# One graph layer and one graph-attention layer on one core: x1 is transposed on VectorE and through DRAM instead of on TensorE, the third weight product moves into the front part, and GpSimd's sums get a fixed order

## The chip, the cores and the metric

The kernel runs on one core of one Trainium2 chip. The metric is the device time of one execution in microseconds (us); less is better. The engines are called PE (TensorE, the matrix engine; PEld are its weight loads), DVE (VectorE), ACT (ScalarE), POOL (GpSimd) and SP (SyncE, which here issues all DMAs). Each engine works through its own queue in order. Which instruction stands where in a queue is decided when the program is built.

## The reference

There are 64 graphs of 256 nodes with 512 features, all fp32. Two layers follow each other, each with a residual and a layer norm:

```
h  = relu(adj @ (x @ W1) + b1)
h  = relu(adj @ (h @ W2) + b2)
x1 = layernorm(x + adj @ (h @ W3) + b3)

q, k = split(x1 @ Wqk);  v = x1 @ Wv
agg  = adj @ (k * mask)
w    = mask * sum(q * agg, -1) / sqrt(512)        # one number per node
out  = layernorm(x1 + softmax(w)[:, None] * v)
```

The kernel never forms q and k. With M = Wq Wk' it uses sum(q * agg) = sum((x1 M) * (adj (mask x1))), so that the second layer needs one weight product with M, one with Wv, and one product of the adjacency with mask * x1.

## The kernel before

**Tiling.** Two graphs (G = 2) are worked on together; there are 32 such pairs. A pair's features or nodes lie on the 128 partitions. Every large product is cut into 2 x 2 blocks and done with seven block products instead of eight. `seven` (L95) holds the schedule of one such group: the products are issued in the order 1, 7, 6, 2, 5, 3, 4 into three PSUM banks called x (products 1, 6, 5, 3 add up in it), v (7 and 4) and y (2). Between the products ACT copies partial results out of x (t1 after product 1, u after 6, q after 5), and DVE adds a bank and a copy into the four output blocks (c11 after 2, c22 after 5, c21 after 4; c12 after 3 is an ACT copy or a DVE add). The operands of products 3, 5, 6 and 7 include sums of blocks:

- `a_sums` (L207) makes four sums S of blocks of the left operand on POOL, 128 x 512 each. Product 7 needs S[2]; product 6 needs S[1], which is made from S[0].
- `b_sums` (L80) makes four sums T of blocks of the right operand, also 128 x 512: for weights once on DVE, for data on POOL. Product 7 needs T[2]; product 6 needs T[1], which is made from T[0].

**Stages of one pair.** `support` (L219) is a weight product: 28 matmuls (56 passes on PE, since each fp32 matmul is two) of 128 x 256, on line L227. `aggregate` (L233) multiplies by the adjacency without the seven-product trick: 32 passes into four PSUM banks (L240), each emptied by one ACT instruction with bias and relu (L243) into a feature chunk of hT. `adj_times` (L257) multiplies by the adjacency with seven products (28 passes, L265). `front` does support 1, aggregate 1, support 2, aggregate 2. `back` does support 3, `adj_times` on its result C, the residual and the layer norm into r (this is x1), then 16 transposes of 128 x 128 on PE (L352) with four ACT copies (L353) to get x1T, then xm = mask * x1 on ACT (L359, four instructions), `adj_times` on xm into gt, and for each of the two graphs `attention` (L367): seven products of 128 x 512 against Wv and M with lhsT blocks of x1T or of its sums S, and the score w on DVE. `finish` (L394) waits for the softmax of w, forms the output on DVE (two fused multiply-adds and a layer norm per graph) and stores it.

**Order of the work.** `run` (L402) interleaves front of pair i with back of pair i - 1: both are generators, the one with fewer steps so far goes next, and `yield 8` (L346) after the layer norm of r keeps back still for eight steps of front. The instructions then go through a list scheduler that fills each engine's queue by priority and by its own estimate of when operands are ready, for all five engines. `softmax_rows`, `softmax_cols` and `finish` of pair i - 2 are called at the start and in the middle of support 3 of pair i - 1.

**Buffers.** PSUM has eight banks in one rotation. On-chip buffers of interest: S 6, act (hT and x1T) 5, r 2, x (shared by x and xm) 1, gt 1, v 3, T 4, tmp 6.

## Time and profile before

| | us |
|---|---|
| median of 3 runs (2920.73 to 2921.39) | 2920.84 |
| the profiled execution | 2920.62 |
| its span, first to last instruction | 2918.8 |
| PE busy in the span | 2883.0 (99%) |
| POOL / DVE / ACT busy | 1346.4 / 1009.2 / 911.4 |
| one pair in the steady part, start to start | 89.37 |

A row "PE MATMUL ... x28" stands for 28 passes, and its time runs from the first start to the modelled end of the last; the distance from one row's start to the next row's start is what PE really took. An idle time in brackets at the end of a row is that of the engine just before it, with what ended it. The steady part consists of 31 equal periods: the first pair alone (with the making of M) takes until 68.45, the periods until 2838.9, and the last pair's back, with nothing beside it, takes the rest.

### The profile page before, as it was taken

How to read it: one execution, taken by the hardware profiler on the slowest of the kernel's cores; microseconds unless marked ns; L12 is line 12 of the kernel's file. 1: busy time of each engine (PE TensorE's matmuls, PEld its weight loads, DVE VectorE, ACT ScalarE, POOL GpSimd, SP SyncE). 2: the span in 40 equal slices, each digit the busy share in tenths (PEclk: the TensorE clock that was granted, in tenths of full speed). 3: DMA queues.
4: the chain of work that ended last, by engine and by line, in shares of the span. 5: the costliest groups of instructions: out<-in, count | busy, mean ns of one | idle time of the engine just before them, and what ended most of it. 6: DMA issues, size and time to landing. Idle time of an engine off the chain costs nothing. (4 is left out here: it accounts for less than half of the span.)

```text
span 2918.8 us, 30346 instructions
## 1 busy us (share of the span) xinstructions
PE 2883.0 (99%) x11776; PEld 2150.7 (74%) x11776; DVE 1009.2 (35%) x2126; ACT 911.4 (31%) x1574; POOL 1346.4 (46%) x1130
## 2 busy tenths in 40 slices
PE   8999999999999999999999999999999999999996
PEld 7787777877777777778777787777787777877773
DVE  2233323333333333233333333332333333333325
ACT  2332333323333323333223333233332323332332
POOL 5534445444455344544444543545444445435442
PEclk9999999999999999999999999999999999999999
DMA  4101101111011011010110110110101101101000
GB/s 149 37 29 51 51 22 51 42 39 51 22 51 51 29 51 45 28 51 32 48 51 22 51 51 29 51 38 35 51 29 51 51 22 51 51 29 51 37 15 29
DMA packets 28719, 126.01 MB, mean 43 GB/s; under 512 B 3232, under 2 KB 6432, under 8 KB 20384
## 3 DMA queue, kind: packets, MB, share of 16 engines
q1 hardware_dynamic: 28576, 124.08, 11.7%
q8 instruction: 93, 1.52, 0.2%
q14 instruction: 50, 0.41, 0.0%
HBM read 90.51 MB, written 33.55 MB: 43 GB/s over the span
## 5 line engine op out<-in xcount | busy, mean ns | idle before, releaser
L227 PE MATMUL ps<-w_T,S 128*128 128x256 f32 x2304 | 524.0, 379 | 2.2 <-DVE w_T L85 1.6
L227 PEld LDWEIGHTS ps<-w_T,S 128*128 128x128 f32 x2304 | 437.5, 190 | 63.1 <-POOL S L61 2.7
L240 PE MATMUL ps<-aT,sup 128*128 128x256 f32 x2048 | 484.0, 381 | 0.0
L240 PEld LDWEIGHTS ps<-aT,sup 128*128 128x128 f32 x2048 | 386.4, 190 | 61.8 <-DVE sup L58 10.6
L373 PE MATMUL ps<-mv_T,S 128*128 128x512 f32 x768 | 350.5, 592 | 0.0
L58 DVE TENSOR_TENSOR sup<-ps,tmp 128x512 f32<-128x512 f32 x288 | 194.1, 683 | 441.1 <-PE ps L227 396.8
L243 ACT ACTIVATE hT<-ps,b 128x512 f32<-128x512 f32 x256 | 176.0, 688 | 441.6 <-PE ps L240 441.6
L111 ACT COPY tmp<-ps 128x512 f32<-128x512 f32 x224 | 131.3, 586 | 523.9 <-PE ps L227 290.8
L373 PEld LDWEIGHTS ps<-mv_T,S 128*128 128x128 f32 x768 | 145.9, 190 | 183.7 <-issue 168.6
L102 ACT COPY tmp<-ps 128x512 f32<-128x512 f32 x224 | 130.2, 581 | 401.4 <-PE ps L227 212.0
L119 ACT COPY tmp<-ps 128x512 f32<-128x512 f32 x224 | 130.7, 584 | 399.1 <-PE ps L373 180.5
L373 PE MATMUL ps<-v,x1T 128*128 128x512 f32 x512 | 251.0, 592 | 0.0
L227 PE MATMUL ps<-w,hT 128*128 128x256 f32 x1024 | 245.2, 382 | 0.0
L83 POOL TENSOR_TENSOR T<-sup 128x512 f32<-128x512 f32 x32 | 40.7, 1271 | 436.3 <-ACT sup L229 436.3
L61 POOL TENSOR_TENSOR S<-hT 128x512 f32<-128x512 f32 x128 | 162.5, 1270 | 144.7 <-PE ps L373 104.7
L58 DVE TENSOR_TENSOR v<-ps,tmp 128x512 f32<-128x512 f32 x128 | 88.5, 691 | 405.5 <-PE ps L373 405.5
L58 DVE TENSOR_TENSOR gt<-ps,tmp 128x512 f32<-128x512 f32 x96 | 66.4, 692 | 414.2 <-PE ps L265 388.6
L227 PEld LDWEIGHTS ps<-w,hT 128*128 128x128 f32 x1024 | 189.6, 190 | 24.5
L58 DVE TENSOR_TENSOR r<-ps,tmp 128x512 f32<-128x512 f32 x96 | 65.3, 680 | 407.6 <-PE ps L265 270.5
L265 PE MATMUL ps<-T,aS 128*128 128x256 f32 x768 | 197.0, 386 | 3.5 <-POOL T L85 3.5
L227 PE MATMUL ps<-w,S 128*128 128x256 f32 x768 | 179.1, 382 | 1.5 <-ACT tmp L119 0.8
L83 POOL TENSOR_TENSOR T<-xm 128x512 f32<-128x512 f32 x32 | 40.8, 1274 | 285.4 <-ACT xm L359 277.5
(94 smaller groups left out, 4059.0 us busy)
## 6 DMA issues: line engine op xcount, KB each, us to landing
xT<-in_xT SPq DMA_DIRECT2D x32, 1024.0 KB, 4.7
x<-in_xN SPq DMA_DIRECT2D x32, 1024.0 KB, 4.8
out<-v SPq DMA_DIRECT2D x64, 512.0 KB, 2.6
aT<-in_adjT SPq DMA_DIRECT2D x32, 512.0 KB, 5.4
w<-in_W SPq DMA_DIRECT2D x9, 256.0 KB, 5.2
wqT<-in_WqT SPq DMA_DIRECT2D x4, 256.0 KB, 5.2
wkT<-in_WkT SPq DMA_DIRECT2D x4, 256.0 KB, 5.0
v<-in_Wv SPq DMA_DIRECT2D x2, 512.0 KB, 6.4
```

Source lines behind the costliest of these rows:

```text
L58: nc.vector.tensor_tensor(o, a, b, op=OP.add)
L61: nc.gpsimd.tensor_tensor(o, a, b, op=op)
L83: eng.tensor_tensor(Ts[0], B[1], B[0], op=sub)
L102: nc.scalar.copy(t1, x)
L111: nc.scalar.copy(u, x)
L119: nc.scalar.copy(q, x)
L227: nc.tensor.matmul(ps[:, g], lhsT=src[n](c, g), rhs=w[n][:, c], start=(first and g == 0 and c == 0), stop=(g == G - 1 and c == 1), skip_gr ...
L240: nc.tensor.matmul(ps[:, g], lhsT=C[k][c // 2][:, g, (c % 2) * P:(c % 2 + 1) * P], rhs=aT[:, k, g], start=(g == 0 and k == 0), stop=(g == ...
L243: nc.scalar.activation(hT[c // 2][:, c % 2], ps, AF.Relu, bias=b[:, c:c + 1])
L265: nc.tensor.matmul(ps[:, g], lhsT=aS[n][:, g], rhs=mov[n][:, g], start=(first and g == 0), stop=(g == G - 1), skip_group_check=True)
L373: nc.tensor.matmul(ps, lhsT=src[n](c, g), rhs=mv[n][:, c], start=(first and c == 0), stop=(c == 1), skip_group_check=True)
```

## The change

- x1T is no longer made by PE. After the layer norm of each graph, four `nc.vector.transpose` instructions on DVE turn 128 x 256 of r each in blocks of 32 x 32 (eight per pair) into tr. One DMA writes tr (1 MB) to DRAM, four DMAs of 256 KB each read it back into 32 partitions of x1T each. In x1T neighbouring nodes lie 16 elements apart, so the attention's weight loads and the sums S of x1T read with that step. tr shares its one buffer with gt.
- Support 3, the sums of the adjacency (`adj_sums`), the load of x and x + b3 move from back to front; so do the sums S of the next pair's input. Back now begins with the sums T of C, then softmax and finish of the pair before, then `adj_times` on C.
- `run` now counts microseconds: each yield gives a stage's PE time (1.73, 0.86, 1.72), a tuple such as `(14,)` keeps the generator still for that long, and the generator that is further behind relative to 50 or 37 goes next.
- `manual_schedule` takes POOL out of the list scheduler: its queue has the order in which the code issues. In `b_sums` T[2] is made first.
- Buffers: S 11, act 4, r 1, v 2, x1T its own 1; the softmax works in place.

In the built program of the changed kernel DVE has eight `StreamTranspose` per pair, PE no longer has the 16 transposes, and SP has five more DMAs per pair.

```diff
+    dram = ctx.enter_context(tc.tile_pool(name="dram", bufs=2, space=bass.MemoryType.DRAM))
+    ctx.enter_context(tc.manual_schedule(engines={mybir.EngineType.Pool}))
...
     def b_sums(B, Ts, eng):
         sub = OP.subtract
+        eng.tensor_tensor(Ts[2], B[3], B[1], op=sub)
         eng.tensor_tensor(Ts[0], B[1], B[0], op=sub)
         eng.tensor_tensor(Ts[1], B[3], Ts[0], op=sub)
-        eng.tensor_tensor(Ts[2], B[3], B[1], op=sub)
         eng.tensor_tensor(Ts[3], B[2], Ts[1], op=sub)
...
-    def a_sums(hT):
-        S = [pool.tile([P, 2, G, P], FP, name="S", tag="S", bufs=6) for _ in range(4)]
-        blk = lambda h, k: hT[k][:, :, :, h * P:(h + 1) * P]
+    def a_sums(blk):
+        S = [pool.tile([P, 2, G, P], FP, name="S", tag="S", bufs=11) for _ in range(4)]
...
+    def first_sums(hT):
+        return a_sums(lambda h, k: hT[k][:, :, :, h * P:(h + 1) * P])
...
+    def t_sums(B):
         Ts = [pool.tile([P, G, HD], FP, name="T", tag="T", bufs=4) for _ in range(4)]
         b_sums((B[0][0], B[0][1], B[1][0], B[1][1]), Ts, nc.gpsimd)
+        return Ts
...
-    def front(i, hT, aT):
-        C = yield from support(hT, wl[0])
+    def front(i, hT, src, aT):
+        C = yield from support(hT, wl[0], src)
         nxt = load_xT(i + 1) if i + 1 < NPAIR else None
         hT = yield from aggregate(C, aT, bcol[0])
         C = yield from support(hT, wl[1])
         hT = yield from aggregate(C, aT, bcol[1])
-        return hT, nxt
-
-    def back(i, hT, aT, prev):
         x = load_x(i)
-        if prev is not None:
-            sm = softmax_rows(prev[2])
-        src = support(hT, wl[2])
-        for _ in range(3):
-            next(src)
-            yield
+        aS = adj_sums(aT)
+        steps = support(hT, wl[2])
+        for _ in range(4):
+            yield next(steps)
         for g in range(G):
             for h in range(NH):
                 padd(x[:, g, h, :], x[:, g, h, :], b3b)
+        nS = first_sums(nxt) if nxt is not None else None
+        C = yield from steps
+        return C, aS, x, nxt, nS
+
+    def back(i, C, aS, x, prev):
+        Ts = t_sums(C)
+        yield (3.4,)
         if prev is not None:
+            sm = softmax_rows(prev[2])
+            yield (3.4,)
             s = softmax_cols(sm)
             for g in range(G):
                 finish(i - 1, g, prev, s)
-        C = yield from src
-        aS = adj_sums(aT)
-        r = pool.tile([P, G, NH, D], FP, name="r", bufs=2)
+        r = pool.tile([P, G, NH, D], FP, name="r", bufs=1)
...
+        tr = pool.tile([P, 4, 32, NH, 2, 2, G], FP, name="tr", tag="gt", bufs=1)
+        x1T = pool.tile([P, P, NH, 2, 2, G], FP, name="x1T", bufs=1)
         for g in range(G):
             layernorm(r[:, g])
-        yield 8
-        x1T = [pool.tile([P, 2, G, N], FP, name="x1T", tag="act", bufs=5) for _ in range(2)]
-        for c in range(DC):
-            pt = bank()
-            for g in range(G):
-                for h in range(NH):
-                    nc.tensor.transpose(pt[:, g, h * P:(h + 1) * P], r[:, g, h, c * P:(c + 1) * P], ident)
-            nc.scalar.copy(x1T[c // 2][:, c % 2], pt)
-        yield
+            for h in range(NH):
+                for k in range(2):
+                    nc.vector.transpose(tr[:, :, :, h, k, :, g].rearrange("p q j c -> p c q j"),
+                                        r[:, g, h, k * HD:(k + 1) * HD].rearrange("p (c q j) -> p c q j", c=2, q=4))
+        via = dram.tile([4, P, D], FP, name="via")
+        nc.sync.dma_start(via.rearrange("q p e -> p q e"), tr.rearrange("p q j h k c g -> p q (j h k c g)"))
+        for q in range(4):
+            nc.sync.dma_start(x1T[q * 32:(q + 1) * 32].rearrange("p (a j) h k c g -> p a (j h k c g)", a=4),
+                              via[q].rearrange("(a i) e -> i a e", a=4))
+        yield (14,)
         xm = pool.tile([P, G, NH, D], FP, name="xm", tag="x", bufs=1)
...
-        yield from adj_times(aS, xmb, lambda y, t: add(gb(0, 0), y, t), lambda x: nc.scalar.copy(gb(0, 1), x),
+        yield from adj_times(aS, xmb, t_sums(xmb), lambda y, t: add(gb(0, 0), y, t), lambda x: nc.scalar.copy(gb(0, 1), x),
                              lambda v, t: add(gb(1, 0), v, t), lambda v, t: add(gb(1, 1), v, t))
+        src = a_sums(lambda h, k: x1T[:, :, h, k].rearrange("p n c g -> p c g n"))
+        yield (4,)
         for g in range(G):
             yield from attention(g)
...
     def run(*gens):
         res = [None] * len(gens)
-        live = {k: 0 for k in range(len(gens))}
+        done, free = [0.0] * len(gens), [0.0] * len(gens)
+        live = set(range(len(gens)))
+        now = 0.0
         while live:
-            k = min(live, key=live.get)
+            ready = [k for k in live if free[k] <= now] or [min(live, key=lambda k: free[k])]
+            k = min(ready, key=lambda k: done[k] / gens[k][1])
             try:
-                hold = next(gens[k])
-                live[k] += 1 + (hold or 0)
+                us = next(gens[k][0])
...
+            if isinstance(us, tuple):
+                free[k] = now + us[0]
+            else:
+                done[k] += us
+                now += us
...
+            gens.append((front(i, xTs, xS, aT), 50.0))
...
+            gens.append((back(i - 1, *state, prev), 37.0))
```

## The prediction

> **What bounds the kernel now.** I read the page's busy times first, then one steady period engine by engine, then that period's PE timeline.
>
> ```profile
> PE 2883.0 (99%) x11776; PEld 2150.7 (74%) x11776; DVE 1009.2 (35%) x2126; ACT 911.4 (31%) x1574; POOL 1346.4 (46%) x1130
> ```
> ```profile
> 1000.00:1089.37 89.37, 89.37 (x366) 66.67 (x365) 31.05 (x66) 28.30 (x50) 41.67 (x36) 1.00 0.12 42
> ```
> ```profile
> 1012.37 6.39 PE L240 MATMUL ps<-aT,sup 128*128 128x256 f32 x28
> 1018.60 1.91 PE L352 MATMUL ps<-ident,r 128*128 128x128 f32 x16
> 1020.35 1.03 PE L265 MATMUL ps<-xm,aT 128*128 128x256 f32 x4
> ...
> 1028.36 3.60 PE L373 MATMUL ps<-mv_T,S 128*128 128x512 f32 x8
> 1031.79 1.88 PE L373 MATMUL ps<-v,x1T 128*128 128x512 f32 x4
> ...
> 1054.58 7.07 PE L227 MATMUL ps<-w_T,S 128*128 128x256 f32 x32
> 1061.48 1.89 PE L227 MATMUL ps<-w,xT 128*128 128x256 f32 x8
> ```
>
> The second fence is one period (its first columns: length, then PE, PEld, DVE, ACT and POOL busy): PE is busy all through, at full granted clock, and no other engine reaches half. In the third, start to start gives the price of a pass: 6.90 / 32 = 0.216 us at 256 columns, 3.43 / 8 = 0.429 at 512, and the 16 transposes take 1020.35 - 1018.60 = 1.75. A pair has 288 passes of 256 (62.2), 56 of 512 (24.0), the transposes (1.75) and 0.4 of softmax transposes: 88.4 of the 89.37. The other 1.0 is gaps of under 0.1. So PE sets the time, and the change is worth 1.75 us per pair at most, unless PE waits where it did not.
>
> What a wait looks like when nothing stands beside it is seen in the tail, where the last back runs alone:
>
> ```profile
> 2856.26 1.99 PE L265 MATMUL ps<-T,aS 128*128 128x256 f32 x8 [2.25 <-POOL T L85]
> 2873.84 1.99 PE L265 MATMUL ps<-T,aS 128*128 128x256 f32 x8 [1.26 <-POOL T L85]
> ```
>
> There PE stands still for POOL's sums T. In the steady part front's products cover them. The prices of the waiting chain are in the groups by shape (mean ns after the busy time) and in POOL's and DVE's timelines:
>
> ```profile
> L243 ACT ACTIVATE hT<-ps,b 128x512 f32<-128x512 f32 x256 | 176.0, 688 | 441.6 <-PE ps L240 441.6
> L61 POOL TENSOR_TENSOR S<-hT 128x512 f32<-128x512 f32 x128 | 162.5, 1270 | 144.7 <-PE ps L373 104.7 <-ACT hT L243 40.0
> L359 ACT ACTIVATE xm<-r,mask_t 128x512 f32<-128x512 f32 x128 | 85.3, 714 | 6.5 <-DVE r L285 5.8 <-issue 0.7
> L285 DVE TENSOR_SCALAR r<-r,mv,rs 128x512 f32<-128x512 f32 x128 | 63.9, 541 | 1.2
> L83 POOL TENSOR_TENSOR T<-xm 128x512 f32<-128x512 f32 x32 | 40.8, 1274 | 285.4 <-ACT xm L359 277.5 <-PE ps L352 7.9
> ```
> ```profile
> 996.79 1.27 POOL L61 TENSOR_TENSOR S<-hT 128x512 f32<-128x512 f32 x1 [0.52 <-ACT hT L243]
> 998.14 1.27 POOL L61 TENSOR_TENSOR S<-S,hT 128x512 f32<-128x512 f32 x1
> 999.49 1.27 POOL L61 TENSOR_TENSOR S<-hT,S 128x512 f32<-128x512 f32 x1
> ```
> ```profile
> 1064.02 0.15 DVE L309 COPY s<-ps 128x4 f32<-128x4 f32 x1
> ...
> 1071.28 0.99 DVE L285 TENSOR_SCALAR v<-v,mv,rs 128x512 f32<-128x512 f32 x2
> ```
>
> A sum on POOL takes 1.27, and 1.35 when it needs the one before. One pair's finish holds DVE from 1064.02 to 1072.19, 7.5 without the block add inside it.
>
> **The sum without new waits.** The period would be 89.37 - 1.75 = 87.62. Moving support 3 takes 56 x 0.216 = 12.1 from the tail to the first pair: that ends at 81 instead of 68.45. The tail was 2918.8 - 2838.9 = 79.9. It loses support 3 and 3.6 of transposes, and gains the exposed round trip (about 30 us from the last front to x1T, of which the layer norm, PE's product with xm and softmax were there before): I count 76. Total 81 + 76 + 31 x (87.62 + S) = 2873 + 31 S, where S is the wait that a period gains, and 1.8 more for the device time (2920.62 against 2918.8; the profiled run lies 0.2 under the median). The kernels tie at S = 1.5.
>
> **Part by part.**
>
> *Queue order after the aggregate of layer 1.* I set t = 0 at the first pass of `adj_times` on C, and count PE by its queue in the built program. The fourth aggregate bank ends at 16.4. Behind it PE has only: support 2 product 1 (to 18.1), 7 (19.9), 6 (21.6), then xm product 1 (22.5), 7 (23.3), and xm product 6, which needs T[1]. POOL's fixed queue between that bank and T[1] is S[0], S[1], S[3], T[2], T[0], T[1]: 6 x 1.27 + 3 x 0.08 = 7.85. With 0.26 from PE's last pass to ACT (1031.79 in the PE rows, copied from 1032.05), 0.69 of ACT and 0.15 of hand-overs, T[1] is ready 8.95 after the bank, PE comes to it after 6.9. That is 2.05 of wait with nobody late. Before, the 1.75 of transposes and other products stood in this place.
>
> *xm ahead of the bank on ACT.* ACT's queue reads: xm(half 0, graph 0), bank 3, xm(half 0, graph 1), bank 4, two more xm. So bank 4 waits for the layer norm of graph 1, and that for DVE. DVE's queue from t = 0.26: finish 7.5, one block add and the first add of r 0.6 each, to 9.0; three adds of r and one block add, 11.45; statistics and normalizing of graph 0, 3.7, to 15.15 (1005.45 to 1008.98 in the old order, with two statistics already done); four transposes at X each; 0.55 to the first half of graph 1. xm then ends at 16.4 + 4X and bank 4 at 17.1 + 4X.
>
> *X, a DVE transpose of 128 x 256.* The trace has none. From below, half of the 541 ns row, 0.27; from above half of POOL's 1270 ns, 0.64; the last resort is a whole 512-element DVE sum at its slowest (w_T, 1212 ns), 1.2, for the writes lie 64 bytes apart. I take 0.40, near the rows that read or write 512 elements at 680 (0.34), with some start-up. Bank 4 leaves at 18.75, T[1] is ready at 26.65, PE starts xm product 6 at 26.75 instead of 23.33: 3.4. About 0.3 of the period's gaps fall before it and are swallowed: S = 3.1. X = 0.27 gives 2.6, 0.64 gives 4.1, 1.2 gives 6.3.
>
> The Trainium skill, "VectorE: DVE Perf Modes", § The three transpose paths and its rules, speaks against this step: it puts a 128 x 128 bf16 transpose at 311 ns on VectorE and advises TensorE where PSUM will do. Two of those are 0.62, S = 4.0 and 2999 us by it; no row here decides.
>
> *Softmax.* PE's row transposes now stand 3.8 before the column transposes. The chain between took 3.2 (1052.63 to 1055.84); 0.2 of slack, no wait. If a copy cuts in on ACT, 0.6 per pair.
>
> *Round trip.* The transposes end at 16.2 + 8X = 19.4. The write of 1 MB: between the 2.6 of a 512 KB store and the 5.4 of the slowest load in the page's DMA list; I take 5. The four reads: between 4.7 (1 MB in one) and 4 x 5.2 in turn; they are issued together, I take 6. x1T lands at about 31. It is needed with S[1] of x1T (3.9 later) at 38 + 3.1 = 41: 6 us to spare, at the upper ends 8 too late. Behind the write on SP stand the reads and the next x and aT, wanted 30 us later; behind x1T's sums on POOL the sums for support 3, wanted at 62. DVE's first gt add, at 28, waits for tr to be read out, at 24.4.
>
> *Strided x1T.* Weight loads take 190 ns under passes of 429: nothing, unless more than doubled (24 loads per pair). POOL's sums could take up to twice 1.27 and still be in time. The skill's "GPSIMD Engine Reference", § Performance pitfalls for Q7 kernels, gives half again for steps over 8 bytes: 5.7 instead of 3.9, no change in the sum.
>
> *Rest.* DVE's two-input sums beside POOL could slow finish (w_T rows: 857 alone to 1212), up to 1.1 on S; taken as 0. The one r buffer is free before its first add, as finish stands earlier on DVE. Four ACT copies per pair fall away (2.4 of an engine a third busy).
>
> Forecast: 2873 + 31 x 3.1 + 1.8 = 2971.
>
> **Rivals.**
> 1. *Faster: the sums come in time.* PE waits for T[1] less than 1.5 per period, because the small gaps and stretched earlier passes give POOL its 2 us. For it: the old steady part has no wait over 0.1 under the same scheduler. Against: POOL is no longer in that scheduler, and both counts start at the same bank. S = 0 gives 2875, S = 1 2906.
> 2. *Only POOL's chain counts*: DVE is a microsecond quicker than counted, and bank 4 leaves at once. S = 2.05 - 0.3, 2928.
> 3. *The turn itself is late*: transposes near 1.2, the reads one after the other, or weight loads over 429. S from 5 to 9: 3030 to 3154.
>
> That the transposes stay on PE is excluded by the built queue.
>
> **How the numbers follow.** Forecast (S 2.3 to 4.6, 2946 to 3017) 0.55; rival 1 0.17; rival 2 (S 1.5 to 2.3, 2921 to 2946) 0.14; rival 3 0.14. Within 0.2% (5.8 us, about what this measurement can tell from no change) lie S 1.3 to 1.7: 0.01 of rival 1 and 0.04 of rival 2. So faster 0.16, same 0.05, slower 0.79. The range leaves out 0.12 of rival 1 below 2905 and 0.08 of rival 3 above 3045; the likeliest case's own is 2946 to 3017.
>
> **What would show it.** A period of 90.7; PE idle before L274 passes on T, ended by POOL, and before L233 passes on S, about 3 together per pair; `StreamTranspose` near 400 ns; x1T landing 5 us or more before the attention. Wrong, if the period is under 89, if the idle time is ended by a DMA, or if the passes on x1T start later than 0.43 apart.

## The result and the profile after

The changed kernel takes 3008.82 us (median of 4 executions, 3006.86 to 3009.1) against 2921.11 (2920.73 to 2922.55): a ratio of 1.0298, with a 95% interval of 1.028 to 1.0316. The forecast was 2971, with a range of 2905 to 3045. The sign is right, and the loss is 88 us where 50 were forecast. The profiled execution took 3006.86, with a span of 3005.1.

The page's busy times of the kernel after, and one of its steady periods (length, then PE, PEld, DVE, ACT and POOL busy, granted clock, share of the DMA engines, GB/s):

```profile
PE 2858.7 (95%) x11264; PEld 2164.8 (72%) x11264; DVE 1238.2 (41%) x2382; ACT 859.8 (29%) x1446; POOL 1439.1 (48%) x1130
```
```profile
1557.68:1649.38 91.70, 88.37 (x349) 67.00 (x348) 38.53 (x74) 26.71 (x45) 44.70 (x35) 1.00 0.20 64
```

PE lost its 512 transposes and 24 us of busy time, and fell from 99% to 95% of the span. The period grew from 89.37 to 91.70 at full clock. 31 periods make 72 us of the loss. The other 14 lie in the first pair and the tail (the last pair's back, with nothing beside it): 3005.1 - 31 x 91.70 = 162.4, where before it was 2918.8 - 31 x 89.37 = 148.3.

PE's timeline of the kernel after, in the same period, with the rows behind which PE stood still and a few beside them:

```profile
1568.90 1.13 PE L274 MATMUL ps<-T,aT 128*128 128x256 f32 x4 [0.97 <-DVE r L61]
1569.87 6.21 PE L246 MATMUL ps<-aT,sup 128*128 128x256 f32 x28
1575.92 1.89 PE L233 MATMUL ps<-w,hT 128*128 128x256 f32 x8
1577.64 1.89 PE L233 MATMUL ps<-w_T,S 128*128 128x256 f32 x8
1581.21 1.97 PE L233 MATMUL ps<-w_T,S 128*128 128x256 f32 x8 [1.68 <-ACT tmp L105]
1583.02 1.03 PE L274 MATMUL ps<-xm,aT 128*128 128x256 f32 x4
1583.88 2.09 PE L274 MATMUL ps<-T,aS 128*128 128x256 f32 x8
...
1593.70 1.99 PE L233 MATMUL ps<-w,S 128*128 128x256 f32 x8 [0.68 <-ACT tmp L122]
1595.54 1.89 PE L233 MATMUL ps<-w_T,hT 128*128 128x256 f32 x8
1597.26 1.88 PE L385 MATMUL ps<-v,x1T 128*128 128x512 f32 x4
```

Three waits stand where there were none. Product 4 of `adj_times` on C waits for DVE to read r's block out of the bank. Product 6 of support 2 waits for ACT's copy t1, which must leave bank x before product 6 may be written there. Product 3 of support 2 waits for the copy q, since it follows product 5 on PE with nothing between. PE's first pass on x1T, the last row, waits for nothing. In the kernel before, four passes of aggregate 2 (L240) stood between the products 5 and 3:

```profile
1006.19 1.89 PE L227 MATMUL ps<-w_T,S 128*128 128x256 f32 x8
1007.92 1.03 PE L240 MATMUL ps<-aT,sup 128*128 128x256 f32 x4
1008.85 1.96 PE L227 MATMUL ps<-w,S 128*128 128x256 f32 x8
```

From start to start and less the price of the passes, the three waits of the kernel after are 1.14, 1.85 and 0.84 per period. Gaps of under 0.15 make 1.16 more (before: 1.00, and nothing else).

The rest of the reading is on the other three engines. ACT in the kernel after, from the fourth bank of aggregate 1 (L249) to t1 (L105):

```profile
1576.12 0.69 ACT L249 ACTIVATE hT<-ps,b 128x512 f32<-128x512 f32 x1
1578.46 0.72 ACT L372 ACTIVATE xm<-r,mask_t 128x512 f32<-128x512 f32 x1 [1.66 <-DVE r L294]
1579.88 0.72 ACT L372 ACTIVATE xm<-r,mask_t 128x512 f32<-128x512 f32 x1 [0.69 <-DVE r L294]
1580.50 0.57 ACT L105 COPY tmp<-ps 128x512 f32<-128x512 f32 x1
```

The bank left at once; t1 stood behind two xm that waited for the layer norm of the second graph. POOL:

```profile
1576.88 1.27 POOL L64 TENSOR_TENSOR S<-hT 128x512 f32<-128x512 f32 x1 [1.75 <-ACT hT L249]
...
1583.51 1.27 POOL L88 TENSOR_TENSOR T<-xm,T 128x512 f32<-128x512 f32 x1
```

T[1], the second row, ends at 1584.78, which is 8.86 after the aggregate (1575.92); the prediction's chain gave 8.95. PE reaches its first pass on T[1] at about 1584.8, so this chain ends just when PE, freed by t1, gets there. DVE, with the normalizing of v in `finish` and of r's two graphs (L294), and its transposes (L360):

```profile
1564.17 2.50 DVE L294 TENSOR_SCALAR v<-v,mv,rs 128x512 f32<-128x512 f32 x2
...
1567.26 0.99 DVE L294 TENSOR_SCALAR v<-v,mv,rs 128x512 f32<-128x512 f32 x2
...
1573.48 1.94 DVE L294 TENSOR_SCALAR r<-r,mv,rs 128x512 f32<-128x512 f32 x2
1575.33 1.93 DVE L360 STREAM_TRANSPOSE tr<-r 128x256 f32<-128x256 f32 x4
...
1577.32 2.52 DVE L294 TENSOR_SCALAR r<-r,mv,rs 128x512 f32<-128x512 f32 x2
1579.76 1.92 DVE L360 STREAM_TRANSPOSE tr<-r 128x256 f32<-128x256 f32 x4
```

The same pair of instructions takes 0.99 when POOL rests and 2.50 beside two of POOL's sums. The groups by shape in the kernel after (busy time, then mean ns of one, then idle time before):

```profile
L385 PEld LDWEIGHTS ps<-v,x1T 128*128 128x128 f32 x512 | 143.3, 294 | 52.2 <-issue 10.5
L294 DVE TENSOR_SCALAR r<-r,mv,rs 128x512 f32<-128x512 f32 x128 | 137.5, 1115 | 1.9
L64 POOL TENSOR_TENSOR S<-x1T 128x512 f32<-128x512 f32 x64 | 131.8, 2080 | 227.6 <-DMA x1T<-via 227.6
...
L360 DVE STREAM_TRANSPOSE tr<-r 128x256 f32<-128x256 f32 x256 | 123.3, 587 | 0.0
```

Normalizing r went from a mean of 541 to 1115 ns.

### The profile page after: what moved, and what is told of

The parts are those of the page before. It is cut to its first block, busy times and chain, and to the rows that moved or that the text cites. A ratio compares the mean times of both kernels' runs of the same rounds, so it can differ in the third digit from the quotient of the medians.

```text
span 3005.1 us, 30012 instructions
## 1 busy us (share of the span) xinstructions
PE 2858.7 (95%) x11264; PEld 2164.8 (72%) x11264; DVE 1238.2 (41%) x2382; ACT 859.8 (29%) x1446; POOL 1439.1 (48%) x1130
## 4 chain that ended last, share of the span: by engine, by line
PE 72%; DVE 20%; issue 3%; ACT 1%; POOL 0%; DMA 0%; SPq 0%; DVEq 0%; POOLq 0%; ACTq 0%
PE ps L233 30%; PE ps L385 26%; PE ps L274 8%; PE ps L246 7%; DVE st L283 5%; DVE r L294 4%; DVE v L411 3%; DVE v L294 2%; DVE tr L360 2%; DVE r L61 1%; DVE mv L284 1%; DVE sup L61 1%; ACT tmp L122 1%; ACT tmp L105 1%; POOL S L64 0%
## 5 line engine op out<-in xcount | busy, mean ns | idle before, releaser
L233 PE MATMUL ps<-w_T,S 128*128 128x256 f32 x2304 | 538.5, 381 | 53.4 <-ACT tmp L105 50.5
L64 POOL TENSOR_TENSOR S<-hT 128x512 f32<-128x512 f32 x128 | 162.2, 1268 | 799.9 <-ACT hT L249 799.9
L246 PE MATMUL ps<-aT,sup 128*128 128x256 f32 x2048 | 473.2, 379 | 1.6 <-DVE sup L61 1.6
L385 PE MATMUL ps<-mv_T,S 128*128 128x512 f32 x768 | 356.9, 594 | 0.3 <-POOL S L64 0.3
L249 ACT ACTIVATE hT<-ps,b 128x512 f32<-128x512 f32 x256 | 175.2, 685 | 510.5 <-PE ps L246 510.5
L64 POOL TENSOR_TENSOR tmp<-tmp,x 128x512 f32<-128x512 f32 x96 | 134.7, 1417 | 281.5 <-ACT tmp L105 203.8
L385 PE MATMUL ps<-v,x1T 128*128 128x512 f32 x512 | 241.6, 594 | 2.0 <-DMA x1T<-via 2.0
L64 POOL TENSOR_TENSOR S<-x1T 128x512 f32<-128x512 f32 x64 | 131.8, 2080 | 227.6 <-DMA x1T<-via 227.6
L105 ACT COPY tmp<-ps 128x512 f32<-128x512 f32 x224 | 130.5, 582 | 297.3 <-PE ps L233 136.5
L274 PE MATMUL ps<-T,aS 128*128 128x256 f32 x768 | 208.0, 399 | 2.2 <-POOL T L88 1.4
L233 PEld LDWEIGHTS ps<-w,S 128*128 128x128 f32 x768 | 143.0, 190 | 63.3 <-ACT tmp L122 33.6
L385 PEld LDWEIGHTS ps<-v,x1T 128*128 128x128 f32 x512 | 143.3, 294 | 52.2 <-issue 10.5
```

What stands on the lines that cost most here:

```text
L64: nc.gpsimd.tensor_tensor(o, a, b, op=op)
L105: nc.scalar.copy(t1, x)
L233: nc.tensor.matmul(ps[:, g], lhsT=src[n][:, c, g], rhs=w[n][:, c], start=(first and g == 0 and c == 0), stop=(g == G - 1 and c == 1), skip ...
L246: nc.tensor.matmul(ps[:, g], lhsT=C[k][c // 2][:, g, (c % 2) * P:(c % 2 + 1) * P], rhs=aT[:, k, g], start=(g == 0 and k == 0), stop=(g == ...
L249: nc.scalar.activation(hT[c // 2][:, c % 2], ps, AF.Relu, bias=b[:, c:c + 1])
L274: nc.tensor.matmul(ps[:, g], lhsT=aS[n][:, g], rhs=mov[n][:, g], start=(first and g == 0), stop=(g == G - 1), skip_group_check=True)
```

## The experiments

Each kernel is the changed one with the edit shown, unless it says otherwise. Times are medians, ratios are to the kernel before on the same chip (2920.98 to 2922.15 us), with their 95% intervals. "Wait" means PE's stand from start to start, less the price of the passes.

### One place, several chains

**t1 ahead of the second graph's xm.** The two xm of graph 1 may issue on ACT only after the last t1 copy.

```diff
+    copied = []
-        nc.scalar.copy(t1, x)
+        copied[:] = [nc.scalar.copy(t1, x).ins]
...
-                nc.scalar.activation(xm[:, g, h, :], r[:, g, h, :], AF.Copy, scale=mask_t[:, h, b:b + 1])
+                with tc.issue_after(copied[0]) if g else nullcontext():
+                    nc.scalar.activation(xm[:, g, h, :], r[:, g, h, :], AF.Copy, scale=mask_t[:, h, b:b + 1])
```

> One order on ScalarE is changed and nothing else: the two xm of graph 1 are issued behind the t1 copy of layer 2's weight product, no longer ahead of it. TensorE's 1.68 us of idle time before that product 6 (ended by the t1 copy) should go, since the copy then starts at product 1's end, near 1578.5 instead of 1580.50. Theory A (ScalarE's order is the whole wait in this place): the period falls by the full 1.7, from 91.70 to 90.0, and the time by 31 x 1.7 = 53 us, to about 2956. Theory B (GpSimd's chain S0, S1, S3, T2, T0, T1 ends at the same moment: T[1] is ready at 1584.78 and the idle time only moves down the queue): TensorE now stands still before xm product 6 for T[1] instead, the period stays within 0.2 of 91.70, and the time at 3002 to 3012.

Measured: 3009.63 us, 1.0305 [1.029, 1.0321]. The wait at product 6 of support 2 fell to 0.24, and one of 1.59 came up at the first pass on T[1]. PE's row in this kernel:

```profile
1585.71 1.13 PE L276 MATMUL ps<-T,aS 128*128 128x256 f32 x4 [1.43 <-POOL T L88]
```

ACT's order named the wait but did not carry its size: POOL's chain ends at nearly the same moment.

**POOL's chain shorter by one.** S[3] of support 2, not needed until its product 3, is issued behind the sums T of xm.

```diff
-        padd(S[3], blk(0, 1), S[1], sub)
+        pend.append(lambda: padd(S[3], blk(0, 1), S[1], sub))
+        if not late:
+            pend.pop()()
...
+        xTs = t_sums(xmb)
+        while pend:
+            pend.pop()()
```

> One order on GpSimd is changed: S[3] of layer 2 is made behind the four sums T of xm instead of ahead of them, so T[1] is ready 1.35 us earlier, near 1583.4. Theory B (two waits that end together, ScalarE's t1 copy and GpSimd's T[1]): the copy still holds TensorE to 1581.21, and only the 0.3 that is left before xm product 6 goes: period 91.4, 2999 to 3006 us. A theory that GpSimd's chain alone is the wait: 1.35 less per period, 90.35, and 2967 us.

Measured: 3006.45 us, 1.0293 [1.0278, 1.0309]. PE still waits 1.68 for t1. Removing either chain alone buys next to nothing.

**Both edits together.**

> Both orders are changed at once: t1's copy ahead of graph 1's xm on ScalarE, S[3] behind the sums T on GpSimd. Theory B: each alone gives next to nothing and both together 1.35 to 1.7 per period, for T[1] (near 1583.4) now ends the wait 1.4 earlier: period 90.0 to 90.4, 2956 to 2968 us. Were the two waits independent, the gain would be the sum of the two single ones; if neither matters, the time stays near 3005.

Measured: 3000.98 us, 1.0278 [1.0261, 1.0296], where some 2962 was expected. A wait of 1.40 at T[1] was left. POOL's row shows whom it waits for now:

```profile
1576.80 1.28 POOL L86 TENSOR_TENSOR T<-xm 128x512 f32<-128x512 f32 x1 [1.12 <-ACT xm L384]
```

The first sum of T waits for xm, and xm for DVE's layer norm of graph 1. T[1] ends 8.60 after the aggregate instead of 8.86. That is a third chain with an end close to the others, and the expectation had not counted it.

**The first edit, and back held for 16 us instead of 14.** PE then does more of front's products between support 2 and xm.

```diff
-        yield (14,)
+        yield (16,)
```

> t1's copy goes ahead of graph 1's xm, and the hold is 16 instead of 14, which puts product 2 of layer 2's weight product (1.72 us of TensorE) ahead of the products with xm, in the place where the transposes stood before. GpSimd's order is as in the changed kernel. Theory B: the t1 wait goes and T[1] (1584.78) is met by TensorE's arrival (1579.5 + 1.7 + 1.7 + 0.9 + 0.9 = 1584.7), so the 2.0 of this place go: period 89.7, 2945 us. What is left of S is then about 2 us per period, the wait of product 4 on C (0.97) and the one of product 3 (0.68). If the lost time is not in this place, the period stays above 91.

Measured: 2962.85 us, 1.0145 [1.013, 1.016], period 90.08. Both the t1 and the T[1] waits are gone (0.24 left). Product 4 on C (1.14) and the copy q (0.84) wait as before. So, with t1 freed, two more microseconds of PE work in front of the place cover all three chains at once, which shortening them did not do: -46 us. The longer hold without the first edit was not run.

### The other collision: DVE beside POOL

**POOL back in the list scheduler.**

```diff
-    ctx.enter_context(tc.manual_schedule(engines={mybir.EngineType.Pool}))
```

> Only GpSimd's fixed order is given back to the scheduler. In the place where TensorE waits, its order comes out the same (S[2], S[0], S[1], S[3] of layer 2, then T[2], T[0], T[1], T[3] of xm); elsewhere the sums of x1T, x + b3 and the sums of the adjacency change places. Theory B: same time, 2995 to 3015. A theory that the fixed order on GpSimd costs the time: 2950 or less.

Measured: 2992.07 us, 1.0247 [1.023, 1.0264], a little under what was expected. The wait for t1 stayed at 1.85; product 4 on C waits 0.55 instead of 1.14, and that is the whole gain (the period is 91.13, 0.57 less). POOL's rows, and then DVE's, in the stretch ahead of product 4:

```profile
1554.51 1.56 POOL L63 TENSOR_TENSOR tmp<-tmp,x 128x512 f32<-128x512 f32 x1 [6.73 <-ACT tmp L104]
1556.38 1.60 POOL L63 TENSOR_TENSOR tmp<-tmp,x 128x512 f32<-128x512 f32 x1 [0.31 <-ACT tmp L113]
```
```profile
1556.13 0.72 DVE L410 SCALAR_TENSOR_TENSOR v<-v,s,r 128x512 f32<-128x512 f32 x1
...
1556.86 1.67 DVE L410 SCALAR_TENSOR_TENSOR v<-v,s,r 128x512 f32<-128x512 f32 x1
...
1559.86 0.97 DVE L293 TENSOR_SCALAR v<-v,mv,rs 128x512 f32<-128x512 f32 x2
```

POOL's sums now fall beside a multiply-add, which loses 0.95, and no longer beside the normalizing of v, which had lost 1.5 (0.97 instead of 2.50). Counted from the softmax's column transposes, DVE reaches r's first add after 8.41 instead of 8.99, and PE gains the same. So 0.6 of the 1.14 at product 4 is shown to be the price of DVE and POOL meeting. That the rest is too follows only from the times, since the meeting still costs DVE 0.95 here.

### The turn itself

**The changed kernel with PE's transposes.** Everything else of the change stays.

```diff
-                    nc.vector.transpose(tr[:, :, :, h, k, :, g].rearrange("p q j c -> p c q j"),
-                                        r[:, g, h, k * HD:(k + 1) * HD].rearrange("p (c q j) -> p c q j", c=2, q=4))
-        via = dram.tile([4, P, D], FP, name="via")
...
         yield (14,)
+        for c in range(DC):
+            pt = bank()
+            for g in range(G):
+                for h in range(NH):
+                    nc.tensor.transpose(pt[:, g, h * P:(h + 1) * P], r[:, g, h, c * P:(c + 1) * P], ident)
+            nc.scalar.copy(x1T[:, c], pt)
+        yield 1.75
```

> Only the turn is undone: x1 is turned by 16 TensorE transposes and four ScalarE copies per pair, as before, and everything else of the change stays (layer 3's product and x + b3 in the front part, the new orders). TensorE has 1.75 more to do per period, in the place between layer 2's product 6 and the products with xm. Theory B (two thirds of the loss is the order, a third is the turn): the transposes fill the place in which TensorE now waits for the t1 copy and T[1] (2.0 of idle time become 1.75 of work), DVE is 3.9 us freer, and the wait before product 4 on C (0.97) and before layer 2's product 3 (0.68) stay: period 90.3 to 91.5, time 2955 to 3000, still slower than before. A theory that the DVE and DRAM turn is the whole loss: period back at 89.4 and the time at 2921 or below.

Measured: 3003.87 us, 1.0285 [1.027, 1.0301]. With none of the turn in it, this kernel loses 83 of the 88 us. Its period is 91.92, 0.22 longer than with the turn on DVE, but its ends take 3001.6 - 31 x 91.92 = 152.1 instead of 162.4. It has the 1.14 at product 4 and a wait of 1.39 at support 2's product 7, for S[2]. ACT's rows (L249 is the fourth bank), then PE's:

```profile
1580.33 1.33 ACT L369 ACTIVATE xm<-r,mask_t 128x512 f32<-128x512 f32 x2 [0.73 <-DVE r L294]
1581.57 0.67 ACT L249 ACTIVATE hT<-ps,b 128x512 f32<-128x512 f32 x1
```
```profile
1584.98 1.99 PE L233 MATMUL ps<-w_T,S 128*128 128x256 f32 x8 [1.22 <-POOL S L64]
```

Here the fourth bank does stand behind an xm of the second graph. That is the mechanism of the forecast, in another kernel: the list scheduler set ACT's order anew after the edit.

**The turn alone**, in the kernel before (its support 3, its order of stages, its scheduler); x1T's strided sums and the buffers act 4 and v 2 come with it.

```diff
+    dram = ctx.enter_context(tc.tile_pool(name="dram", bufs=2, space=bass.MemoryType.DRAM))
...
+                    nc.vector.transpose(tr[:, :, :, h, k, :, g].rearrange("p q j c -> p c q j"),
+                                        r[:, g, h, k * HD:(k + 1) * HD].rearrange("p (c q j) -> p c q j", c=2, q=4))
...
-        x1T = [pool.tile([P, 2, G, N], FP, name="x1T", tag="act", bufs=5) for _ in range(2)]
-        for c in range(DC):
...
-        src = a_sums(x1T)
+        src = a_sums(None, lambda h, k: x1T[:, :, h, k].rearrange("p n c g -> p c g n"))
```

> The turn alone, in the kernel before: VectorE transposes, DRAM write and four reads in place of the 16 TensorE transposes and four ScalarE copies; the order of work, the third weight product in the back part and the scheduler's GpSimd order stay as before. To fit SBUF, act has 4 buffers instead of 5 and v 2 instead of 3. In the old period (1000.00 as its start) r's layer norm ends near 1010, the transposes near 1012, x1T lands some 12 us later (1581.7 to 1593.7 in the changed kernel), so near 1024.0, and TensorE reaches the attention at 1024.83 - 1.75 + 1.75 of slack at most, near 1023 to 1025. Theory D (the turn is good for most of its 1.75, the move of layer 3's product and the new order cost the time): gaps grow by 1.0 at most, period 87.7 to 88.7, and the time 2885 to 2915 with 3 to 6 us more in the tail. A theory that the round trip is what costs: TensorE waits for x1T or the sums on it by 2 us or more per period, 2930 to 3000.

Measured: 3092.03 us, 1.0583 [1.0567, 1.0599], where a gain was expected. POOL's rows, then PE's, then three stretches of 2 us (columns as in the period above; the clock is the third column from the end):

```profile
1550.52 1.42 POOL L62 TENSOR_TENSOR aS<-aT 128x256 f32<-128x256 f32 x2 [8.38 <-PE ps L267]
...
1553.38 4.02 POOL L62 TENSOR_TENSOR S<-x1T 128x512 f32<-128x512 f32 x2
```
```profile
1555.61 5.43 PE L378 MATMUL ps<-mv_T,S 128*128 128x512 f32 x8 [2.59 <-POOL S L62]
```
```profile
1555.60:1557.60 2.00, 1.99 (x3) 0.96 (x4) 0.00 (x0) 0.00 (x0) 1.92 (x2) 0.50 0.43 180
1557.60:1559.60 2.00, 2.00 (x5) 0.52 (x4) 0.00 (x0) 0.00 (x0) 1.92 (x2) 0.68 0.00 0
1559.60:1561.60 2.00, 2.00 (x6) 1.25 (x5) 0.00 (x0) 0.47 (x1) 2.00 (x2) 1.00 0.00 0
```

The scheduler put the sums of the adjacency (aS), whose buffer comes free only with the last product on aS, ahead of x1T's sums. POOL stood still for 8.38 with the x1T sums behind. PE waited 2.75 for S[2]; then its granted clock was 0.50 and 0.68 in the next two stretches, and passes of 0.43 took up to twice that: 1.83 more. These slow passes cost nothing, though. In the period before this one the clock stayed at 1.00 after the same wait, and PE stood again, for S[1]:

```profile
1461.50 1.98 PE L378 MATMUL ps<-mv_T,S 128*128 128x512 f32 x4 [2.59 <-POOL S L62]
1465.01 1.98 PE L378 MATMUL ps<-mv_T,S 128*128 128x512 f32 x4 [1.53 <-POOL S L62]
```

That period is 94.11 long, the next, with the slow passes, 94.04. Only where the clock fell after the second wait is a period clearly longer, 96.3 to 96.4: six of the 28 periods from 230.93 to 2880.

**The turn alone, with x1T's sums first on POOL.**

```diff
-        aS = adj_sums(aT)
+        with tc.issue_after(summed[0]) if summed else nullcontext():
+            aS = adj_sums(aT)
```

> The turn alone in the kernel before, as in the run at 3092 us, with one GpSimd order changed: the adjacency's four sums, which wait until TensorE has used the last ones, are issued behind the sums on x1T instead of ahead of them. In that run the adjacency's sums held GpSimd from 1550.52 to 1553.38 while x1T had landed near 1549, and TensorE waited 2.75 for S[2] and then ran passes at half speed for 1.8 more. If this order is the cause, both go: period 89.4 to 89.8 from 94.04, time 2950 to 2965, still above the kernel before by the 0.78 (before layer 2's product 4) and 0.84 (before xm product 4) that TensorE's transposes covered. If x1T itself is late (the round trip not hidden), the wait for S[2] stays above 1.5 and the time above 3010.

Measured: 2967.74 us, 1.0156 [1.0139, 1.0173], 3 us above what was expected: 124 us of the loss just seen were that order, with some 15 (an estimate, from the lengths of the periods) for the clock. The period is 90.59 in the middle (a mean of 90.65). Three waits are left:

```profile
1568.89 1.99 PE L233 MATMUL ps<-w_T,hT 128*128 128x256 f32 x8 [0.63 <-DVE sup L59]
...
1582.36 1.13 PE L271 MATMUL ps<-xm,aS 128*128 128x256 f32 x4 [0.68 <-ACT tmp L120]
...
1588.64 1.98 PE L383 MATMUL ps<-mv_T,S 128*128 128x512 f32 x4 [0.86 <-POOL S L62]
```

The first (0.78 from start to start) is for a block add of support 2 that stands behind four of the transposes on DVE (1566.36 to 1568.15). The second (0.86) is for a copy q that PE's first passes on x1T covered before, and the third (1.1) for S[1] of x1T, which landed 11.3 after the last transpose. With small gaps they outweigh the 1.75 that PE saved. So in the old order the turn costs DVE's time as well as about a microsecond of lateness on the way through DRAM and the strided sums. The ends take 2966.5 - 31 x 90.65 = 156.3, 8 more than before. The new order gives x1T the time it needs; it pays for that elsewhere.

### Looking for a version that gains

**The layer norm of v behind r's.** `finish` is split into its multiply-adds, which stay, and its layer norm, which is issued behind the transposes and xm. r's layer norm is held behind the last add of layer 1's support; back waits 14 us in the first kernel and 18 in the second, 2 of them ahead of the layer norm. The xm of graph 0 are held behind the aggregate's last bank, those of graph 1 behind t1, as in the first edit.

```diff
-                finish(i - 1, g, prev, s)
+                mix(g, prev, s)
...
+        if prev is not None:
+            with tc.issue_after(turned.ins), tc.issue_after(masked.ins):
+                for g in range(G):
+                    norm_out(i - 1, g, prev)
```

> finish is split: v x s + r stays ahead of the first add of r on VectorE, the layer norm of v and the store go behind the turn of r. The adds of x1's layer norm no longer stand behind the two normalizings of v that took 2.50 us beside a GpSimd sum. xm is issued behind layer 1's last bank on ScalarE, that of graph 1 behind the t1 copy, so that no copy waits for r. Theory C (VectorE's lateness costs the 0.97 before product 4 on C): that wait goes and only that; T[1] still ends the wait in layer 2 (1.4 to 1.7) as in the run with the t1 copy first, and 0.68 before product 3 stays: period 90.5 to 90.8, time 2968 to 2980. A theory that VectorE's lateness is the root of all waits: period 88.5 or less, 2908 or less.

> The same as the split of finish, with the hold at 18 instead of 14: products 2 and 5 of layer 2 also go ahead of the products with xm, so that T[1] is asked for 3.4 us later, and product 3 no longer follows product 5 at once. All waits named so far should go (0.97 + 2.0 + 0.68): period 88.0 to 88.4, time 2890 to 2905, faster than before the change by 0.5 to 1%. If new waits come (x1T or the sums on it later than the attention asks for them, since the attention now follows at once behind layer 2's first aggregate bank), the idle time before the passes on x1T, ended by POOL S or by a DMA, shows it.

Measured: 3033.94 us, 1.0398 [1.0374, 1.0423], and 2990.45 us, 1.0238 [1.0222, 1.0253]. The wait of product 4 on C fell to 0.67 and no further, though no normalizing of v stands ahead of it any more; there DVE waits for a POOL sum. The wait for T[1] disappeared, but the square roots of v's layer norm (L288) now stand on ACT ahead of a copy that PE needs. ACT's rows and then PE's in the second kernel:

```profile
1574.92 0.30 ACT L288 ACTIVATE sd<-mv,eps 128x2 f32<-128x2 f32 x1 [2.97 <-DVE mv L286]
1575.71 0.30 ACT L288 ACTIVATE sd<-mv,eps 128x2 f32<-128x2 f32 x1 [0.50 <-DVE mv L286]
1575.92 0.56 ACT L116 COPY tmp<-ps 128x512 f32<-128x512 f32 x1
```
```profile
1576.53 1.99 PE L235 MATMUL ps<-w_T,S 128*128 128x256 f32 x8 [1.85 <-ACT tmp L116]
```

The two square roots wait for DVE, the copy behind them leaves only at 1575.92, and PE stands for 2.02. In the first kernel (its profiled execution took 3048.18) another copy is held in the same way, for 2.52 of PE, and in 16 of 28 periods the clock falls to 0.50 behind it. Such a period is 93.8 to 93.9 long, one without the fall 92.4.

**Three edits together**: t1 ahead, POOL in the scheduler, back held for 18 us.

> The changed kernel with three orders mended: the t1 copy ahead of graph 1's xm on ScalarE, the hold at 18 instead of 14 (products 2 and 5 of layer 2 ahead of the products with xm, so that T[1] has 3.4 us more, and product 3 no longer at once behind product 5), GpSimd's order by the scheduler. What is left of TensorE's idle time: 0.4 to 0.6 before product 4 on C, 0.25 before layer 2's product 6, and 1.1 to 1.2 in gaps under 0.15, as in the runs that had each alone. Period 88.4 to 88.8, time 2903 to 2918. If a new wait comes (sums on x1T later than the attention, which now follows about 2 us earlier), it stands before the passes on S of x1T and is ended by GpSimd or a DMA; then 2920 to 2960.

Measured: 2928.83 us (10 executions), 1.0028 [1.0018, 1.0037]. This is the nearest to the kernel before, and still slower; 2903 to 2918 was expected. Beside the waits foreseen, one of 0.52 came up at aggregate 2, for a block add of support 2. Its period is 89.18, 0.19 shorter than before's 89.37, which is worth 6 us in 31 periods. But its first pair and tail take 2925.3 - 31 x 89.18 = 160.7 against 148.3. In the steady part it gains a tenth of the 1.75 that PE no longer spends, and the ends cost 12 us. This kernel with PE's transposes was not run, so what the turn itself is worth in this order stays open.

**The same, with the second graph's layer norm of v behind C's product.**

```diff
-            for g in range(G):
-                finish(i - 1, g, prev, s)
+            finish(i - 1, 0, prev, s)
+            mix(1, prev, s)
...
+        if prev is not None:
+            norm_out(i - 1, 1, prev)
```

> The kernel with three orders mended (t1 copy first, hold 18, GpSimd by the scheduler; 2928.83 us) and one edit more: the layer norm and store of the second graph's v are emitted behind the adds of r instead of ahead of them, so that the add which frees TensorE's bank before product 4 on C no longer stands behind two normalizings (0.99 us). Theory C (VectorE's order costs the 0.56 that is left there): that wait goes, period 88.5 to 88.7 from 89.18, time 2908 to 2914, faster than before the change by 0.2 to 0.5%. If the norm of r, now 1 us later, makes xm and T[1] late, up to 0.5 per period comes back before xm product 6 and the time stays at 2920 to 2930.

Measured: 2950.29 us, 1.0099 [1.0084, 1.0114], 21 us worse than without the edit. Product 4's wait fell as meant (0.37), and ACT's third bank of the aggregate came to stand behind an xm. ACT's rows, then PE's:

```profile
1545.77 0.72 ACT L376 ACTIVATE xm<-r,mask_t 128x512 f32<-128x512 f32 x1 [1.13 <-DVE r L295]
1546.39 0.67 ACT L250 ACTIVATE hT<-ps,b 128x512 f32<-128x512 f32 x1
```
```profile
1551.22 1.99 PE L234 MATMUL ps<-w_T,S 128*128 128x256 f32 x8 [0.98 <-POOL S L63]
```

No version found here beats the kernel before.

## Why the prediction was right or wrong

The forecast's sum was 157 + 31 x (87.62 + 3.1). Measured were 162.4 + 31 x (87.62 + 4.08). Of the 36 us that are missing in the span, 30 are S and 5 the ends. The size of S is near, but it is put together from other terms, and that is luck: the place that the forecast reckoned with gave about half of its 3.4, and two places that it had put at nothing made up for it.

| wait per period | predicted | kernel after |
|---|---|---|
| place behind the aggregate (support 2 to xm) | 3.4 | 1.85 |
| product 4 on C, DVE late | 0, up to 1.1 | 1.14 |
| product 3 of support 2, copy q | not seen | 0.84 |
| gaps under 0.15, against 1.00 before | -0.3 | +0.16 |
| passes | 0 | 0.08 |
| S | 3.1 | 4.07 |

**Passes and bound: right.** PE set the time, its passes kept their prices, and the 1.75 did leave its queue.

**The step that failed: "xm ahead of the bank on ACT".** The prediction read the second xm in ACT's queue as graph 1's and let the fourth bank wait for it. It was the second half of graph 0: the bank left at once (1576.12, 0.2 after PE's last pass). Graph 1's xm stand one instruction later, ahead of t1, and hold that up instead. The place therefore cost 1.85 and not 3.4. Of the signs that the prediction named, a stand ahead of the passes on S came, but ended by ACT; one ahead of the passes on T, ended by POOL, did not. The mechanism exists, as the kernel with PE's transposes shows, but not here.

**"Queue order": right, and near to rival 2.** The chain through POOL gave 8.95 to T[1] and a wait of 2.05 with nobody late; measured were 8.86, and 1.59 where t1 was freed. Rival 2 priced this place at 2.05 - 0.3 = 1.75 (which gives 2929, not 2928). Its price was nearer than the forecast's there, and the bank did leave at once. But it had DVE a microsecond quicker, where DVE was slower, it did not see t1, which ended the wait, and it lacked the other two places. That the chain of ACT and that of POOL end together was not seen, nor that a third one, DVE's layer norm to xm to T, ends there too. Hence the small worth of the single edits (0, -2 and, both together, -8 us).

**"Rest", the term taken as 0: wrong.** The prediction named the slowing of DVE beside POOL, gave it up to 1.1, and left it out. The wait for DVE at product 4 on C is 1.14, 35 us in all, of which about half is shown to come from the slowing. The prediction took the row of 857 ns for sums that run alone; it is a mean of three, one of them beside POOL, and alone such a sum takes 0.68, so the slowing was larger than it read. It looked at two-input sums alone; the largest loss fell on the one-input normalizing (0.99 to 2.50). By the rows above, DVE loses 1.5 in v's normalizing, 0.9 in r's first graph and 0.6 until the first half of the second; that these 3 us are also what makes graph 1's xm, and so t1, late follows from the times, but no run took them away by themselves.

**Copy q, not seen.** In the kernel before, aggregate 2's passes stood between products 5 and 3 of support 2, so that the copy was covered. In the changed kernel product 3 stands directly behind product 5. The price could be read in the old profile, in the tail, where product 3 of support 3 had nothing ahead of it:

```profile
2849.37 1.97 PE L227 MATMUL ps<-w,S 128*128 128x256 f32 x8 [0.77 <-ACT tmp L119]
```

This wait costs 26 us.

**X, the DVE transpose: near.** Four take 1.79 to the next instruction, 0.45 each, where 0.40 was taken. The Trainium skill's "VectorE: DVE Perf Modes", § The three transpose paths, puts a 128 x 128 bf16 transpose at 311 ns; the estimate of 0.62 made from it was too much here. That its 2999 us is close to 3008.82 is chance: it comes from a wait at the fourth bank that did not happen. The transposes do stand in the chain to t1, since four of them run on DVE ahead of the second graph's normalizing (1575.33 to 1577.12), but POOL's own chain, which ends with it, does not contain them.

**Round trip and strides: right.** The write was issued after the last transpose (1581.71) and landed 4.4 later; the reads landed at 1593.72, 12.0 after the transposes against 11 counted, and 3.5 before the attention's first pass (1597.26), where 5 or more had been named. Strided weight loads take 294 ns against 190 and stay under passes of 429. x1T's sums take 2080 and POOL has the time. In the old order it has not, and there rival 3's kind of lateness appears. Softmax brought no wait (the slack by the prediction's own numbers, 3.8 - 3.2, is 0.6, not 0.2).

**The ends.** The first pair's first pass on C starts at 86.74 where 81 was counted, and the tail takes 77.3 where 76 was. That is 7 by these marks, 5 by the steady period; ahead of the first mark 24 passes of the next pair (5.2) are already done. Of the 14 us that the ends lost against the kernel before, the kernel with PE's transposes loses only 4 (152.1 against 148.3). The other 10 come with the turn: from the first pass on C to the end the tail takes 66.8 there and 77.3 here. How they divide between DVE's transposes, the way through DRAM (PE waits 2.0 for x1T in the tail) and the clock (a mean of 0.77 instead of 0.85) was not taken apart.

**The part at fault.** With the turn on DVE the new structure costs 88 us, with PE's transposes 83. In the steady part the turn replaced 1.75 of PE's work by nearly as much waiting and gained 0.22 per period, 7 us; in the tail it lost 10. The rest of the loss is that of the new order of stages. This holds for these queues only: the two kernels differ in ACT's order as well.

## What to carry to other kernels

When work leaves the bound engine, list every in-order chain (one per engine and copy) that ends within the time set free, and price all of them: the longest names the wait, the next one sets what removing it is worth. Read each queue again after every edit, down to which tile an instruction belongs to; five of the experiments lost time to an order that the scheduler made anew on ACT or POOL. Covering a place with more work of the bound engine was worth more (46 us, with t1 freed) than shortening single chains. A turn through DRAM that the steady part hides is paid for where nothing stands beside it, here with about 10 us in the tail.

## What the runs showed of the hardware

**DVE and POOL stop each other.** Two normalizing instructions of 512 elements took 0.99 alone and 2.50 beside two POOL sums; a multiply-add 0.72 and 1.67, and in the row above it ends 0.55 after the POOL sum that had begun before it. POOL loses as well: 1.56 and 1.60 instead of 1.27 where a multiply-add had begun first. Transposes did not suffer (four in 1.93 with POOL mostly idle, in 1.92 beside its sums). The Trainium skill's "SBUF — State Buffer", § SBUF: two separate sides, says that DVE and GpSimd share a pair of ports which one instruction holds to its end, whichever starts first, while the other is blocked; on DVE's side it names instructions with two inputs in SBUF and those in a two-port mode. The multiply-adds and POOL's sums agree with that in their starts and ends. Whether the normalizing ran in such a mode no run here shows.

**PE's clock can fall after a stand of 2.5 us.** After waits of up to 1.85 in the kernel after the granted clock stayed at 1.00 in the steady part, and so it did after 29 stands of 2.0 in the kernel with `finish` split and 18 us of hold; one of 2.16 there brought it down. After 2.75 in the turn alone it was 0.50 and back at 1.00 some 4 us later, but in 8 of 28 periods it stayed at 1.00; after 2.52 in the split with 14 us of hold it fell in 16 of 28. The mean over the span was 0.980 and 0.986, against 0.994. The skill's "TensorE: Matmul & The Clock Gate", § HAM oscillation, advises against idle gaps of over about 3.4 us; here 2.6 and less were enough, in some periods. What a fall costs depends on what comes next: 1.4 to 1.5 us in that split, nothing in the turn alone where PE would have waited for S[1] anyway, and 2.2 to 2.3 there (96.3 to 96.4 against 94.1) where the fall came behind that second wait.

**Strides.** A POOL sum with two operands 64 bytes apart per element took 2080 ns against 1268, one with a single such operand 1514; a weight load with that step took 294 against 190.
